# A gated mixture-of-experts layer on one core: input transposes one product earlier, the first matrix looked up early, and silu as one ScalarE function

## The chip, the cores and the metric

The kernel runs on one core of one Trainium2 chip. A core has five engines that run side by side, each with its own queue of instructions taken in order: TensorE (PE in the profile) multiplies matrices and transposes, VectorE (DVE) and ScalarE (ACT) work element by element, GpSimd (POOL) issues the gathers and scatters here, and SyncE (SP) issues the plain transfers. An engine that waits for another one's result holds up everything behind it in its own queue. The metric is the device time of one execution in microseconds (us); less is better.

## The reference, cut to what matters

```python
# x: 4 x 512 tokens of 512 values; ctx: 4 experts, each one 512 x 512 matrix
n = layernorm(x)
e = token_id // 6250, at most 3                 # each token has one of 4 experts
g = silu(n @ ctx[e].T)                          # silu(z) = z * sigmoid(z)
u = n @ ctx[e].T                                # the same matrix: u is the z of the line above
x = x + tanh(g_xattn) * ((g * u) @ ctx[e].T)    # and once more the same matrix

n = layernorm(x)
p = softmax(n @ wr.T)                           # 8 routes
gates = the two largest of p, divided by their sum
h = silu(n @ w1.T); h = silu(h @ w3.T); h = h @ w2.T
out = zeros; out[index of route k] += gate_k * h
x = x + tanh(g_ffn) * out
```

The rows of `out` are indexed by route number (0 to 7) and not by token, so the second half touches only the first eight rows of x. It still has to run over all 2048 tokens, because every token adds to those eight rows.

## The kernel before, in words

**Sorting the tokens.** The 2048 tokens are ordered by expert, so that 128 tokens (one pass) can be multiplied by one expert's matrix. A chain of small VectorE operations on `cum`, `hot`, `incl`, `size`, `cut`, `padded`, `lanes` and `what` finds each token's place in that order. Sixteen small matmuls then turn the places into `tok`, and `from_row` says which row of x each place of each pass takes. This is the position chain. There are 17 passes: 13 use one matrix each, and four, the ones numbered 13 to 16, are split into four groups of 32 rows with a matrix for each group. `matrix_table(n0, n1)` works out from `cut` which matrix each pass or group needs and puts it into `which`; the matrix of a pass can only be loaded once SyncE has read its entry of `which`.

**One pass of the expert half.** Each step below is a function of the kernel and takes the pass number:

- `gather(p)`: GpSimd collects the 128 rows of x into the tile `x` (256 KB).
- `load(p)`: SyncE reads `which` and loads the matrix `m` (1 MB), or four of them.
- `centre(p)`: VectorE takes mean and variance (`st`, `mv`) and subtracts the mean, giving `h_a`. `scale(p)` works out the inverse root `rs` by nine tiny VectorE operations. `norms(p_in, p_out)` does both for a later pass `p_in` together with the second normalization (`h_f`) of an earlier pass `p_out`.
- `turn_in(p)`: TensorE transposes `h_a` into `tp_a`, and ScalarE copies that out of PSUM as `hT`.
- `up(p)`: TensorE multiplies `hT` by the matrix into `z`; the activation is then applied and gives `g`.
- `turn_mid(p)`: TensorE transposes `g` into `tp_g`, ScalarE copies it as `gT`.
- `down(p)`: TensorE multiplies `gT` by the same matrix into `y`; VectorE adds it to `x`, and GpSimd scatters the rows back.
- `turn_out(p)`: TensorE transposes `h_f` into `tp_f`; ScalarE copies that into `hT2`, the input of the second half.

In `up`, the before kernel uses three operations, since g * u is sigmoid(z) * z * z:

```python
nc.scalar.activation(g, z, AF.Sigmoid, scale=rs)
nc.vector.scalar_tensor_tensor(g, z, rs, g, ALU.mult, ALU.mult)
nc.vector.scalar_tensor_tensor(g, z, rs, g, ALU.mult, ALU.mult)
```

**The second half.** `ffn(b)` works on a block of 512 tokens, as a generator that hands back control after each product. It makes four products `u` (by w1), the routing product `lg`, `route` (VectorE, with two small ScalarE sigmoids), four products `v` (by w3), and then `acc`, which adds up gate times h over all tokens. The last block feeds `accT` and finally `o`, the product by w2.

**Order of the work.** Nothing is scheduled automatically: the order in which the code issues is the order in each engine's queue. The main loop runs over i, the passes in the order `order`, and in each turn issues the product z of pass i, the product y of pass i - 1, the transpose of pass i - 2 for the second half, up to two pieces of `ffn` by `step()`, `turn_mid` of pass i and `turn_in` of pass i + 1. Until the first block of 512 tokens is complete (turns 2 to 5), `step()` has nothing to give.

**Buffers.** Eight matrices `m`, five tiles `x` (a tile is free again when its scatter has landed), four PSUM tiles for products, three PSUM tiles for transposes, four tiles `h` shared by `h_a` and `h_f`.

Of the kernel before, what the change touches and what calls it, by code (L numbers as in the profile page):

```python
# [8 lines left out]
F32 = mybir.dt.float32  # L9
BF16 = mybir.dt.bfloat16  # L10
F16 = mybir.dt.float16
I32 = mybir.dt.int32
AF = mybir.ActivationFunctionType
ALU = mybir.AluOpType
AX = mybir.AxisListType
# [3 lines left out]
P = 128  # L19
# [5 lines left out]
def tile_gated_moe_ffn(  # L25
# [40 lines left out]
    nc = tc.nc  # L66
    NT, D = x.shape
# [24 lines left out]
    def ct_(shape, dtype, name):  # L92
        return const.tile(list(shape), dtype, tag=name, name=name)
# [136 lines left out]
        nc.vector.tensor_reduce(padded, terms.rearrange("p h e j -> p j (h e)"), AX.X, ALU.add)  # L230
    inpass_i = ct_([P, NJ], I32, "inpass_i")
    nc.vector.tensor_single_scalar(inpass_i, padded, -P, op=ALU.bitwise_and)
    lanes = ct_([P, NJ], BF16, "lanes")
    nc.vector.tensor_sub(lanes, padded, inpass_i)
    atlane = ct_([P, 2, P, H], F16, "atlane")

    def at_lane(h):
# [44 lines left out]
                which[:, n0:n1], stepped[:, :, n0:n1].rearrange("p e n -> p n e"), AX.X, ALU.add  # L282
            )

    matrix_table(0, 2)
    from_row = ct_([P, NP], I32, "from_row")
    nc.vector.tensor_scalar(from_row, tok, -1.0, 0.0, ALU.add, ALU.max)

    first = ct_([P, NU - NF], I32, "first")
    to_row = ct_([P, NP], I32, "to_row")  # L290
# [33 lines left out]
    def moments(xt, name):  # L324
        st = small.tile([P, 6], F32, tag="st", name=f"st_{name}")
        nc.vector.bn_stats(st, xt)  # L326
        mv = small.tile([P, 2], F32, tag="mv", name=f"mv_{name}")
        nc.vector.bn_aggr(mv, st)
        return mv
# [53 lines left out]
    def centre(p):  # L383

        mvs[p] = moments(xs[p], f"a{p}")
        hs[p] = work.tile([P, D], F32, tag="h", bufs=4, name=f"h_a{p}")
        nc.vector.tensor_scalar(hs[p], xs[p], mvs[p][:, 0:1], None, ALU.subtract)  # L387
# [14 lines left out]
    def load(p):  # L402

        n0, n = (p, 1) if p < NF else (NF + (p - NF) * G, G)
        mats[p] = []
        for i in range(n0, n0 + n):
            at = nc.values_load(
                which[0:1, i : i + 1],
                engines=[SP],
                min_val=0,  # L410
                max_val=(E - 1) * D,
                skip_runtime_bounds_check_because="an expert's number, times D",
            )
            m = mp.tile([P, KC, D], F32, tag="m", name=f"m_{i}")
            nc.sync.dma_start(m, ctxT[bass.ds(at, D), :].rearrange("(k p) f -> p k f", p=P))
            mats[p].append(m)

    def expert_product(out_ps, lhs, p):

        n = P // len(mats[p])  # L420
        for k in range(KC):
            for i, m in enumerate(mats[p]):
                nc.tensor.matmul(  # L423
                    out_ps[i * n : (i + 1) * n, :],
                    lhs[:, k * P + i * n : k * P + (i + 1) * n],
                    m[:, k, :],
                    start=(k == 0),
                    stop=(k == KC - 1),
                )

    def up(p):
        z = ps_mm.tile([P, D], F32, tag="mm", name=f"z_{p}")
        expert_product(z, hTs.pop(p), p)
        g = work.tile([P, D], F32, tag="g", name=f"g_{p}")
        rs = rss.pop(p)
        nc.scalar.activation(g, z, AF.Sigmoid, scale=rs)  # L436
        nc.vector.scalar_tensor_tensor(g, z, rs, g, ALU.mult, ALU.mult)  # L437
        nc.vector.scalar_tensor_tensor(g, z, rs, g, ALU.mult, ALU.mult)  # L438
        gs[p] = g

# [21 lines left out]

    def norms(p_in, p_out):

        names, mv = [], []
        if p_out is not None:
            xt = x1s.pop(p_out)
            mv.append(moments(xt, f"f{p_out}"))
            names.append(f"f{p_out}")
        if p_in is not None:  # L470
            mv.append(moments(xs[p_in], f"a{p_in}"))
            names.append(f"a{p_in}")
        rs = inverse_roots(mv, names)
        if p_out is not None:
            h = work.tile([P, D], F32, tag="h", bufs=4, name=f"h_f{p_out}")
            nc.vector.tensor_scalar(h, xt, mv[0][:, 0:1], rs[0], ALU.subtract, ALU.mult)
            hs2[p_out] = h
        if p_in is not None:
            rss[p_in] = rs[-1]
            hs[p_in] = work.tile([P, D], F32, tag="h", bufs=4, name=f"h_a{p_in}")  # L480
            nc.vector.tensor_scalar(hs[p_in], xs[p_in], mv[-1][:, 0:1], None, ALU.subtract)

    def turn_out(p):

# [19 lines left out]
    def route(b, lg):  # L504

        def st(name, shape=(P, TT, NR)):
            return small.tile(list(shape), F32, tag=name, name=f"{name}_{b}")

        def wide(a):
            return a.unsqueeze(2).to_broadcast([P, TT, NR])

        def first_max(src, i):  # L520
            mx = st(f"mx{i}", (P, TT))
            nc.vector.tensor_reduce(mx, src, AX.X, ALU.max)
            oh = st(f"oh{i}")
            nc.vector.tensor_tensor(oh, src, wide(mx), ALU.is_equal)
            nc.vector.tensor_mul(oh, oh, rank)
            rk = st(f"rk{i}", (P, TT))
            nc.vector.tensor_reduce(rk, oh, AX.X, ALU.max)
            nc.vector.tensor_tensor(oh, oh, wide(rk), ALU.is_equal)
            return mx, oh

        lt = small.tile([P, TT, Q], F32, tag="lt", bufs=2, name=f"lt_{b}")
        nc.vector.transpose(lt.rearrange("p t q -> p (t q)"), lg)
        l1 = lt[:, :, 0:NR]
        m1, oh1 = first_max(l1, 1)
        l2 = st("l2")
        nc.vector.scalar_tensor_tensor(l2, oh1, -1e30, l1, ALU.mult, ALU.add)
        m2, oh2 = first_max(l2, 2)
        d = st("d", (P, TT))
        nc.vector.tensor_sub(d, m1, m2)
        p1 = st("p1", (P, TT))  # L540
        nc.scalar.activation(p1, d, AF.Sigmoid)
        p2 = st("p2", (P, TT))
        nc.scalar.activation(p2, d, AF.Sigmoid, scale=-1.0)
        g = small.tile([P, TT, Q], F32, tag="g", bufs=2, name=f"g_{b}")
        nc.gpsimd.memset(g, 0.0)
        nc.vector.tensor_tensor(oh1, oh1, wide(p1), ALU.mult)
        nc.vector.tensor_tensor(oh2, oh2, wide(p2), ALU.mult)
        nc.vector.tensor_add(g[:, :, 0:NR], oh1, oh2)
        return g

    def ffn(b):
# [3 lines left out]
        for m in range(KC):  # L555
            u = ps_mm.tile([P, TB], F32, tag="mm", name=f"u_{b}_{m}")
            for k in range(KC):
                nc.tensor.matmul(  # L558
                    u,
                    w1[:, k, m * P : (m + 1) * P],  # L560
                    hT[:, k, 0:TB],
                    start=(k == 0),
                    stop=(k == KC - 1),
                )
            sg = work.tile([P, TB], F32, tag="sg", name=f"sg1_{b}_{m}")
            nc.scalar.activation(sg, u, AF.Sigmoid)  # L566
            nc.vector.tensor_mul(s1[:, m, :], sg, u)  # L567
            yield
        lg = ps_tp.tile([P, P], F32, tag="tp", name=f"lg_{b}")
        for k in range(KC):  # L570
# [11 lines left out]
        def gated(t):  # L582
            v = ps_mm.tile([P, D], F32, tag="mm", name=f"v_{b}_{t}")
            for k in range(KC):
                nc.tensor.matmul(  # L585
                    v,
                    s1[:, k, t * P : (t + 1) * P],
                    w3[:, k, :],
                    start=(k == 0),
                    stop=(k == KC - 1),  # L590
                )
            s2 = work.tile([P, D], F32, tag="s2", bufs=5, name=f"s2_{b}_{t}")
            nc.scalar.activation(s2, v, AF.Sigmoid)  # L593
            nc.vector.tensor_mul(s2, s2, v)  # L594
            return s2

        def add(t, s2):
# [55 lines left out]
                step()  # L653

    load(order[0])
    load(order[1])
    for i in range(5):
        gather(order[i])
    centre(order[0])
    turn_in(order[0])  # L660
# [5 lines left out]
    wr = load_w(wrT, "wr")  # L666
    load(order[3])
    row_tables()
    centre(order[2])
    scale(order[2])  # L670
    up(order[0])
    turn_in(order[1])
    up(order[1])
    turn_mid(order[0])
    turn_in(order[2])
    down(order[0])
    turn_mid(order[1])
    norms(order[3], order[0])
# [3 lines left out]
    for i in range(2, NP + 2):  # L682
        if i < NP:
            up(order[i])
        if i + 3 < NP:
            gather(order[i + 3])
            load(order[i + 3])
        if i <= NP:
            down(order[i - 1])
        else:  # L690
            step()
        turn_out(order[i - 2])
        if i <= NP:
            norms(order[i + 2] if i + 2 < NP else None, order[i - 1])
        step()
        running += [ffn(b) for b in range(NB) if last[b] == i - 2]
        if i < NP:
            turn_mid(order[i])
        if i + 1 < NP:
            turn_in(order[i + 1])  # L700
        step()
    while running:
        step()
# [58 lines left out]
```

## Time and profile before

| | |
|---|---|
| time, median of 3 runs | 299.35 us (299.25 to 299.53) |
| span of the profiled execution | 297.4 us |
| TensorE busy | 271.3 us, 91% |
| VectorE busy | 158.4 us, 53% |
| ScalarE busy | 64.1 us, 22% |
| GpSimd busy | 38.6 us, 13% |
| granted TensorE clock | 0.993 |
| moved by DMA | 42.54 MB, mean 143 GB/s |

The span is the time from the first to the last instruction on the core; the run's time is about 2 us more. Busy shares are averages over the whole span, and this kernel has stages that differ: a start of about 20 us in which TensorE has hardly anything to do, the turns without pieces of the second half, a long middle with them, and an end that is only the second half. So the shares alone don't tell what a change is worth. The chain of waits that ended last and the idle time in front of each group are of more use.

The main groups on TensorE are z (63.6 us), y (61.8 us), u (57.0 us) and v (57.1 us), each made of 128 x 512 products. On VectorE the activation's two multiplications in `up` take 12.7 and 12.8 us, those of the second half 11.0 us each.

### The profile page before, as it was taken

What the parts mean: (1) busy time and instruction counts of PE and PEld (TensorE: products, weight loads), DVE (VectorE), ACT (ScalarE), POOL (GpSimd) and SP (SyncE); (2) the same over time, 40 slices, a digit from 0 to 9 for tenths busy, and PEclk for the clock granted to TensorE, in tenths of its full rate; (3) what the DMA queues carried; (4) which work ended last, traced back from release to release, by engine and by line L of the source; (5) the groups of instructions that cost most, each with busy time, mean ns of one, the idle gap of its engine ahead of it and who ended that gap; (6) DMA issues with size and microseconds to landing.
All of it is one profiled execution on the core that took longest, in us unless ns stands there. A gap on an engine that the chain in (4) does not pass through costs nothing.

```text
span 297.4 us, 3491 instructions
## 1 busy us (share of the span) xinstructions
PE 271.3 (91%) x1150; PEld 125.8 (42%) x1150; DVE 158.4 (53%) x610; ACT 64.1 (22%) x125; POOL 38.6 (13%) x61
## 2 busy tenths in 40 slices
PE   0148989889999999999999999999999999999994
PEld 0123444445453535443435444435443444344443
DVE  5368486877472866463755487363635543112411
ACT  1012330322121222131212221212312122111210
POOL 5420111222111111120211111010101100000000
PEclk9999999999999999999999999999999999999997
DMA  0385999994251419751429654125000000000000
GB/s 1 132 327 191 393 392 393 390 322 160 99 178 35 181 43 357 272 176 37 176 59 390 240 181 133 55 109 206 35 2 36 10 2 0 0 0 0 2 0 3
DMA packets 20722, 42.54 MB, mean 143 GB/s; under 512 B 2143, under 2 KB 2207, under 8 KB 20704
## 3 DMA queue, kind: packets, MB, share of 16 engines
q1 hardware_dynamic: 17664, 33.66, 31.6%
q0 software_dynamic: 2720, 8.65, 8.2%
q8 instruction: 9, 0.15, 0.2%
q14 instruction: 9, 0.07, 0.1%
q10 hardware_dynamic: 320, 0.01, 0.1%
HBM read 38.10 MB, written 4.47 MB: 143 GB/s over the span
## 4 chain that ended last, share of the span: by engine, by line
PE 88%; ACT 4%; issue 3%; DMA 2%; POOL 1%; DVE 1%; ACTq 0%; POOLq 0%
PE z L423 21%; PE y L423 20%; PE v L585 19%; PE u L558 19%; PE tp_f L366 3%; DMA x<-in_x_dram,from_row 2%; PE tp_a L366 2%; PE tp_g L366 2%; PE lg L573 1%; ACT hT L399 1%; PE acc L598 1%; ACT hT L490 1%; ACT gT L444 1%; POOL lane L142 1%; PE o L712 0%
## 5 line engine op out<-in xcount | busy, mean ns | idle before, releaser
L423 PE MATMUL z<-m,hT 128*32 128x512 f32 (+1 forms) x232 | 63.6, 604 | 4.4 <-ACT hT L399 4.4
L423 PE MATMUL y<-m,gT 128*32 128x512 f32 (+1 forms) x232 | 61.8, 596 | 0.4 <-ACT gT L444 0.4
L558 PE MATMUL u<-hT,w 128*128 128x512 f32 x128 | 57.0, 594 | 0.2 <-ACT hT L490 0.2
L585 PE MATMUL v<-w,s 128*128 128x512 f32 x128 | 57.1, 595 | 0.0
L423 PEld LDWEIGHTS z<-m,hT 128*32 128x32 f32 (+1 forms) x232 | 23.6, 148 | 37.5 <-issue 31.3
L423 PEld LDWEIGHTS y<-m,gT 128*32 128x32 f32 (+1 forms) x232 | 23.1, 145 | 36.7 <-issue 36.1
L558 PEld LDWEIGHTS u<-hT,w 128*128 128x128 f32 x128 | 23.4, 190 | 26.7 <-issue 26.2
L585 PEld LDWEIGHTS v<-w,s 128*128 128x128 f32 x128 | 23.4, 190 | 26.6 <-issue 24.7
L453 POOL DMA_INDIRECT out_dram<-x,to_row x17 | 16.9, 997 | 119.5 <-DVE x L452 118.9
L437 DVE SCALAR_TENSOR_TENSOR g<-z,rs_a,g 128x512 f32<-128x512 f32 x17 | 12.7, 750 | 33.0 <-ACT g L436 33.0
L594 DVE TENSOR_TENSOR s<-s,v 128x512 f32<-128x512 f32 x16 | 11.0, 686 | 30.4 <-ACT s L593 30.4
L375 POOL DMA_INDIRECT x<-in_x_dram,from_row x17 | 16.6, 977 | 74.4 <-issue 19.5
L567 DVE TENSOR_TENSOR s<-sg,u 128x512 f32<-128x512 f32 x16 | 11.0, 686 | 28.2 <-ACT sg L566 28.2
L452 DVE SCALAR_TENSOR_TENSOR x<-y,tg,x 128x512 f32<-128x512 f32 x17 | 12.8, 751 | 23.4 <-PE y L423 23.4
L436 ACT ACTIVATE g<-z,rs_a 128x512 f32<-128x512 f32 x17 | 11.7, 687 | 47.4 <-PE z L423 47.4
L566 ACT ACTIVATE sg<-u 128x512 f32<-128x512 f32 x16 | 9.6, 599 | 47.3 <-PE u L558 47.3
L366 PE MATMUL tp_a<-ident,h_a 128*128 128x128 f32 x68 | 10.7, 282 | 8.2 <-DVE h_a L387 8.2
L593 ACT ACTIVATE s<-v 128x512 f32<-128x512 f32 x16 | 9.6, 598 | 39.2 <-PE v L585 39.2
L490 ACT COPY hT<-tp_f 128x512 f32<-128x512 f32 x13 | 7.6, 586 | 43.3 <-PE tp_f L366 43.3
L326 DVE BATCH_NORM_STATS2 st_a<-x 128x6 f32<-128x512 f32 x17 | 11.3, 666 | 7.0 <-DMA x<-in_x_dram,from_row 7.0
L438 DVE SCALAR_TENSOR_TENSOR g<-z,rs_a,g 128x512 f32<-128x512 f32 x17 | 12.8, 751 | 0.6
L399 ACT COPY hT<-tp_a 128x512 f32<-128x512 f32 (+1 forms) x18 | 10.2, 573 | 13.2 <-PE tp_a L366 13.2
(132 smaller groups left out, 205.3 us busy)
## 6 DMA issues: line engine op xcount, KB each, us to landing
m<-in_ctxT_dram SPq DMA_DIRECT2D x29, 1024.0 KB
w<-in_w1T_dram SPq DMA_DIRECT2D x1, 1024.0 KB
w<-in_w3T_dram SPq DMA_DIRECT2D x1, 1024.0 KB
w<-in_w2T_dram SPq DMA_DIRECT2D x1, 1024.0 KB
x<-in_x_dram,from_row POOLq DMA_INDIRECT x17, 6.1
out_dram<-x,to_row POOLq DMA_INDIRECT x17, 5.3
wr<-in_wrT_dram SPq DMA_DIRECT2D x1, 64.0 KB
x_first<-out_dram SPq DMA_DIRECT2D x4, 4.0 KB
```

The lines of the kernel that those rows point to most:

```text
L326: nc.vector.bn_stats(st, xt)
L366: nc.tensor.transpose(tp[:, k * P : (k + 1) * P], h[:, k * P : (k + 1) * P], ident)
L375: nc.gpsimd.indirect_dma_start(out=xt, out_offset=None, in_=x, in_offset=bass.IndirectOffsetOnAxis(ap=from_row[:, p : p + 1], axis=0),)
L399: nc.scalar.copy(hT[:, i * n : (i + 1) * n], tp[:, i * n : (i + 1) * n])
L423: nc.tensor.matmul(out_ps[i * n : (i + 1) * n, :], lhs[:, k * P + i * n : k * P + (i + 1) * n], m[:, k, :], start=(k == 0), stop=(k == KC ...
L436: nc.scalar.activation(g, z, AF.Sigmoid, scale=rs)
L437: nc.vector.scalar_tensor_tensor(g, z, rs, g, ALU.mult, ALU.mult)
L438: nc.vector.scalar_tensor_tensor(g, z, rs, g, ALU.mult, ALU.mult)
L452: nc.vector.scalar_tensor_tensor(xt, y, tg[:, 0:1], xt, ALU.mult, ALU.add)
L453: nc.gpsimd.indirect_dma_start(out=out, out_offset=bass.IndirectOffsetOnAxis(ap=to_row[:, p : p + 1], axis=0), in_=xt, in_offset=None, bou ...
L558: nc.tensor.matmul(u, w1[:, k, m * P : (m + 1) * P], hT[:, k, 0:TB], start=(k == 0), stop=(k == KC - 1),)
L585: nc.tensor.matmul(v, s1[:, k, t * P : (t + 1) * P], w3[:, k, :], start=(k == 0), stop=(k == KC - 1),)
```

## The change

There are three parts.

**Transposes.** `turn_in` of the next pass moves from the end of a loop turn to directly behind `up`. For that its input must be there earlier, so the centring of a pass moves out of `norms` and forward by one place (`centre(order[i + 2])` in turn i, on VectorE between the activation of pass i and the addition of y). For the first two passes, `up` takes a function `inside` that is issued before the last quarter of the product: the second pass's `turn_in` goes inside the first z, the first pass's `turn_mid` inside the second z.

**First matrix.** The first pass's matrix number is worked out in two VectorE operations (`start`, `which0`) in the middle of the position chain. The table of the first two entries (`matrix_table(0, 2)`) moves behind `from_row`, and the second matrix is loaded after the first two gathers have been issued in program order.

**Silu.** x * sigmoid(x) becomes one ScalarE function. In `up` this takes away one of the two multiplications on VectorE, in `ffn` the only one after each u and v. The two routing sigmoids become one tanh and two small VectorE operations, since sigmoid(d) = 0.5 + 0.5 tanh(d / 2).

```diff
@@ position chain
+    start = ct_([P, 2 * E - 1], F32, "start")
+    nc.vector.scalar_tensor_tensor(start, cut[:, 1 : 2 * E], 0.0, steps, ALU.is_le, ALU.mult)
     lanes = ct_([P, NJ], BF16, "lanes")
     nc.vector.tensor_sub(lanes, padded, inpass_i)
+    which0 = ct_([P, 1], I32, "which0")
+    with nc.allow_low_precision("whole numbers below 4096"):
+        nc.vector.tensor_reduce(which0, start, AX.X, ALU.add)
...
-    matrix_table(0, 2)
     from_row = ct_([P, NP], I32, "from_row")
     nc.vector.tensor_scalar(from_row, tok, -1.0, 0.0, ALU.add, ALU.max)
+    matrix_table(0, 2)
@@ load
-                which[0:1, i : i + 1],
+                which0[0:1, :] if p == order[0] else which[0:1, i : i + 1],
@@ expert_product, up
-    def expert_product(out_ps, lhs, p):
+    def expert_product(out_ps, lhs, p, inside=None):
...
         for k in range(KC):
+            if k == KC - 1 and inside is not None:
+                inside()
...
-        nc.scalar.activation(g, z, AF.Sigmoid, scale=rs)
-        nc.vector.scalar_tensor_tensor(g, z, rs, g, ALU.mult, ALU.mult)
+        nc.scalar.activation(g, z, AF.Silu, scale=rs)
         nc.vector.scalar_tensor_tensor(g, z, rs, g, ALU.mult, ALU.mult)
@@ norms
-            mv.append(moments(xs[p_in], f"a{p_in}"))
+            mv.append(mvs.pop(p_in))
...
-            hs[p_in] = work.tile([P, D], F32, tag="h", bufs=4, name=f"h_a{p_in}")
-            nc.vector.tensor_scalar(hs[p_in], xs[p_in], mv[-1][:, 0:1], None, ALU.subtract)
@@ route
+        half = st("half", (P, TT))
+        nc.scalar.activation(half, d, AF.Tanh, scale=0.5)
         p1 = st("p1", (P, TT))
-        nc.scalar.activation(p1, d, AF.Sigmoid)
+        nc.vector.tensor_scalar(p1, half, 0.5, 0.5, ALU.mult, ALU.add)
         p2 = st("p2", (P, TT))
-        nc.scalar.activation(p2, d, AF.Sigmoid, scale=-1.0)
+        nc.vector.tensor_scalar(p2, half, -0.5, 0.5, ALU.mult, ALU.add)
@@ ffn
-            sg = work.tile([P, TB], F32, tag="sg", name=f"sg1_{b}_{m}")
-            nc.scalar.activation(sg, u, AF.Sigmoid)
-            nc.vector.tensor_mul(s1[:, m, :], sg, u)
+            nc.scalar.activation(s1[:, m, :], u, AF.Silu)
...
-            nc.scalar.activation(s2, v, AF.Sigmoid)
-            nc.vector.tensor_mul(s2, s2, v)
+            nc.scalar.activation(s2, v, AF.Silu)
@@ start of the work
     load(order[0])
+    for i in range(2):
+        gather(order[i])
     load(order[1])
-    for i in range(5):
+    for i in range(2, 5):
         gather(order[i])
...
+    up(order[0], inside=lambda: turn_in(order[1]))
     centre(order[2])
     scale(order[2])
-    up(order[0])
-    turn_in(order[1])
-    up(order[1])
-    turn_mid(order[0])
+    up(order[1], inside=lambda: turn_mid(order[0]))
     turn_in(order[2])
+    centre(order[3])
     down(order[0])
@@ main loop
         if i < NP:
             up(order[i])
+        if i + 1 < NP:
+            turn_in(order[i + 1])
+        if i + 2 < NP:
+            centre(order[i + 2])
...
             turn_mid(order[i])
-        if i + 1 < NP:
-            turn_in(order[i + 1])
         step()
```

## The prediction

> **What bounds the kernel now.** I read the page's slices first, then who waited for whom, then the chain that ended last, then single engines in order of time.
>
> ```profile
> PE   0148989889999999999999999999999999999994
> DMA  0385999994251419751429654125000000000000
> ```
>
> Each digit is a slice of 7.4 us. TensorE is full from about 75 us to the end. It has holes in slices 1 to 10 only: nothing a faster VectorE or ScalarE does in the middle can count. DMA is full around 35 to 67 us.
>
> ```profile
> PE tp_a L366 <- DVE h_a L387: 8.2, 1, 8.2
> PE z L423 <- ACT hT L399: 4.4, 6, 0.8
> PE acc L598 <- DVE s L594: 0.4, 1, 0.4
> PE y L423 <- ACT gT L444: 0.4, 1, 0.4
> ```
>
> TensorE's own waits (total, times, longest): one long one at the start, six of up to 0.8 us in which z waits for the copy of its transposed input, and two of 0.4 us. Apart from the start, TensorE waits little over 5 us in 297.
>
> ```profile
> 10.57 6.12 DMA x<-in_x_dram,from_row
> ...
> 19.83 5.44 PE z L423 x8
> 25.27 0.02 issue
> 25.30 0.46 ACT g L436
> 25.75 0.13 issue
> 25.88 0.59 ACT hT L399
> 26.47 0.04 issue
> 26.51 3.71 PE z L423 x8
> ...
> 43.91 0.60 ACT hT L399
> 44.52 0.04 issue
> 44.56 3.70 PE z L423 x8
> ...
> 257.19 0.61 ACT s L593
> 257.82 0.70 DVE s L594
> ```
>
> This is the chain that ended last (start, length). The start hangs on the first gather, 6.12 us. From 71 to 212 us the chain is TensorE alone. A product after a wait takes 3.70 us, one without 3.43: 0.27 us is lost to refilling besides the wait. The first z takes 5.44.
>
> ```profile
> 12.00:13.00 1.00, 0.00 (x0) 0.00 (x0) 0.00 (x0) 0.00 (x0) 0.95 (x1) 1.00 0.65 186
> 13.00:14.00 1.00, 0.00 (x0) 0.00 (x0) 0.00 (x0) 0.00 (x0) 0.74 (x1) 1.00 1.04 397
> 15.00:16.00 1.00, 0.00 (x0) 0.00 (x0) 0.00 (x0) 0.00 (x0) 0.69 (x2) 1.00 0.99 361
> ```
>
> The last two columns of the stretches by engine are DMA share and GB/s. From 11 to 16.7 us about 1.65 MB moved (61, 186, 397, 399, 361 and two thirds of 371 KB), though the gathered tile is 0.26 MB: it came in behind the first matrix, 1.05 MB. A gather issued at 90.1 us, with no matrix moving, landed in 3.4 us.
>
> **The Trainium skill.** "ScalarE: Activation LUTs", on what happens when an ACTIVATE runs, has one element per cycle and lane whatever the function, so Silu should cost what Sigmoid does. The trace shows Sigmoid at 599 ns for 512 elements, 687 ns with the scale from a tile; Silu isn't in it. The same page ("What ACT_TABLE_LOAD costs") gives 1283 ns for a load; the trace has two, of 1283 ns each. The changed order has two as well: tanh and Silu share the second, so no switching arises. "DMA: Bandwidth & Descriptors", in "Issuing engines are not separate DMA queues", says transfers from all issuers run on the same 16 engines and interleave; that agrees with the 6.12 against 3.4 us above. "TensorE: Matmul & The Clock Gate", in "What's actually happening", puts an idle array at half clock until about 3.4 us of activity in a free-running window; the first z's weight loads indeed come 0.85 us apart until about 23.3 us and 0.43 after.
>
> **The change part by part.**
>
> *First matrix.* `which` now ends at 9.85 us and the matrix is issued at 10.55, 0.7 later. `which0` would end near 7.2 us, so the issue goes to about 7.9, and at the same delays its megabyte is in by about 12.8. The two added operations (0.17 us each, like their neighbours on `lanes`) stand partly in gaps between dependent neighbours: 0 to 0.2 us on the path, I take 0.1. Moving `matrix_table(0, 2)` behind `from_row` saves nothing, since it ran while `from_row` waited 0.25 us for `tok`. It delays the second matrix to about 11.6 us, which helps: the first gather, issued at 10.65, finds the engines nearly free. Bounds: 3.4 us as at 90.1, landing at 14.05; or mixed with the second matrix, up to 15.2. I take 14.2 against 16.69: gain 2.5 us. The first z follows 3.15 us after landing, as now (16.69 to 19.83), at 17.35. Its matrix is there.
>
> *Second z.* Now 25.27 to 26.51 is 1.24 us, of which the transposes are 0.44. With the transpose inside the first z, ScalarE copies during the last quarter (0.86 us; copy 0.58 plus 0.04). Gain 1.24 - 0.44 + 0.27 = 1.1 us. The second input must be centred by 21.7 us; it should land near 16.
>
> *First y.* Now 30.23 to 31.46, 1.23 us, less two transposes 0.88, plus 0.27: 0.6 us. A new wait eats part: the table load (1.28 us) now stands on ScalarE behind the copy of the second `hT`, so silu of the first pass starts 1 us after its product, and multiplication (0.75) and `tp_g` follow. With the transposes done at 22.05 us: copy to 22.7, load to 23.95, silu to 24.7, multiplication to 25.45, transposes at 25.6, against 25.5 when TensorE gets there. Behind it on VectorE the centring of the third pass (1.42 us) ends near 26.9, when TensorE wants it. So about 0.3 us is lost; gain 0.3 (0 to 0.6).
>
> *Turns 3 to 5.* z waits at 44.56, 53.79 and 63.01, each with 0.78 us idle plus 0.27. Now z, `tp_a` of the next pass, y, `tp_f` and `tp_g` follow without a gap, since `hT` is copied during y: 3.43 + 0.44 + 3.43 + 0.44 + 0.44 = 8.18 us a turn against 9.23. Gain 3 x 1.04 = 3.1 us.
>
> *The last split pass.* z at 215.23 us waits 0.73 because its input's copy queues behind four copies to `hT2`. It will have been copied a turn before. Gain 0.8 with the refill. The 0.24 us wait of u at 223.61 stays: `hT2` is copied in the same place.
>
> *Silu.* 17 multiplications of 0.75 and 32 of 0.69 us leave VectorE, 34.8 us, beside TensorE's work nearly everywhere. On the path are two: before `acc` at 258.56, where u follows 0.7 us sooner; and before the last `accT`, where 0.7 us falls away but `accT` now queues behind the transposes of `a`, which end near 290.75, so it starts there and not at 291.07: 0.3 us. Routing gets two operations of about 0.15 us in place of a ScalarE one; `acc` needs its result over 6 us later.
>
> Sum: 2.5 + 1.1 + 0.3 + 3.1 + 0.8 + 0.7 + 0.3 = 8.8 us, 299.35 - 8.8 = 290.5 us.
>
> **A new wait.** `centre` of pass i + 2 now waits on VectorE for its gather in turn i, ahead of the addition of y. A gather waits for a scatter to free its tile, so the loop is: y added, scatter (6.2 to 6.9 us while DMA is full), gather (6.1 to 6.9), centring. From y added at 31.8 us I get the sixth x at about 45.2, where VectorE would take it at 44.5; the seventh at 53.2 against 52.6. Behind the wait stands the addition of y, whose product ends at 46.8 and 55.0, and the centring takes 1.42. So 0.5 to 0.7 us of waiting fits in, with about a microsecond to spare; from turn 6 a turn takes 15 us and it vanishes.
>
> **The rivals.**
>
> A: the first gather lands no earlier, because the second matrix or the other four gathers take the engines. For it: 6.1 to 6.7 us for all five gathers now. Against it: the bytes that moved before it landed are those of the first matrix. Only the waits go: 299.35 - 6.3 = 293.0.
>
> B: the gather loop becomes the bound in turns 3 to 5, with VectorE late by more than the spare time. For it: DMA full in these slices. Against: the sums above. Losing two thirds of the turns' gain, 2.1 us: 292.6.
>
> C: `tp_a` directly behind z makes TensorE wait in the long middle, where it has no wait now. With 1 us in each of the 11 turns from the seventh on: 290.5 + 11 = 301.5, slower. Against: the centring it needs is a turn old, some 15 us, and VectorE has lost a fifth of its work.
>
> **How the numbers follow.** The forecast 72%, A 12%, B 11%, C 5%. The forecast itself may move by the clock ramp: the first z comes 2.5 us earlier against a free-running window, and could run longer or shorter at half clock, -0.6 to +1.2 us; the gather adds -0.2 to +1.0, the table load 0.3 either way. So 288.7 to 293.3: the forecast's spread with A and B, leaving out C and little of the rest. Faster 0.95 (forecast, A, B), slower 0.04 and the same 0.01, both from C.
>
> **What would show it.** Right: the first gather in under 4.2 us; first z near 17.4 us; no wait of z for `hT` from turn 3 on, products of 3.43 us in the chain; the stretch from the first z to the first u about 47 us in place of 51.5; Silu at 599 and 687 ns. Wrong: a gather still near 6 us (A); VectorE waiting over 1.5 us for x in turns 3 to 5, with y's addition late (B); TensorE waiting for `h_a` after 75 us (C); a third table load.

## The result and the profile after

The changed kernel takes 291.42 us (median of four runs, 291.08 to 293.33) against 299.40 us for the kernel before on the same chip: a ratio of 0.975 [0.971, 0.979]. The profiled span went from 297.4 to 289.6 us, 7.80 us less.

TensorE's row of the page's slices, of the kernel after (a slice is 7.2 us):

```profile
PE   0159999999999999999999999999999999999994
```

The 8s that stood among the first 9s before are gone: TensorE is at 9 from the fourth slice to the last but one. VectorE's busy time fell from 158.4 to 128.8 us.

TensorE's waits after (who waited for whom: total us, times, longest):

```profile
PE tp_a L372 <- DVE h_a L393: 7.0, 1, 7.0
...
PE u L565 <- ACT hT L495: 0.5, 2, 0.2
PE z L431 <- ACT hT L405: 0.5, 1, 0.5
```

Six waits of z for its transposed input (4.4 us) have become one, the first z's. The waits of `acc` and of y are gone. The wait at the start fell only from 8.2 to 7.0. And u now waits twice where it waited once: that one is new.

The chain that ended last, after (start and length in us; x6 is the first six of the eight passes that make a 128 x 512 product; where transposes now stand inside a product they divide it, so the 3.52 us from 23.47 on are the last two passes of the first z and the first six of the second):

```profile
10.75 4.78 DMA x<-in_x_dram,from_row
...
16.50 0.64 DVE h_a L393
...
18.83 4.20 PE z L431 x6
23.04 0.44 PE tp_a L372 x4
23.47 3.52 PE z L431 x8
26.99 0.60 PE tp_g L372 x4
27.60 0.86 PE z L431 x2
28.46 0.54 PE tp_a L372 x4
...
32.87 3.44 PE z L431 x8
...
41.05 3.44 PE z L431 x8
...
57.41 3.44 PE z L431 x8
...
64.72 0.45 PE tp_f L372 x4
65.20 0.59 ACT hT L495
65.83 3.70 PE u L565 x8
69.54 3.43 PE z L431 x8
```

Two readings carry the rest. The four z from 32.87 us on stand 8.18 us apart, products of 3.44 us with one y and nothing else but transposes of 0.44 between them. And the first u at 65.83 is a product of 3.70 us, the mark of one that had to wait: the chain passes through ScalarE's copy `hT` at L495 (the tile that the text calls `hT2`).

Where the 7.80 us of span came from, by the positions of the same instruction in both chains (the difference of one row less that of the row above):

| up to | before | after | gained in this part |
|---|---|---|---|
| first z | 19.83 | 18.83 | 1.00 |
| third z | 35.60 | 32.87 | 1.73 |
| the z behind the first u | 74.96 | 69.54 | 2.69 |
| last split z | 215.23 | 208.95 | 0.86 |
| u behind the third block's `acc` | 259.61 | 252.54 | 0.79 |
| last result, `ob` | 293.89 | 286.09 | 0.73 |

### The profile page after: what moved, and what is told of

Its sections match the earlier page's. It is cut to its first block, busy times and chain, and to the rows that moved or that the text cites. A ratio compares the mean times of both kernels' runs of the same rounds, so it can differ in the third digit from the quotient of the medians.

```text
span 289.6 us, 3462 instructions
## 1 busy us (share of the span) xinstructions
PE 269.1 (93%) x1150; PEld 124.8 (43%) x1150; DVE 128.8 (44%) x571; ACT 63.7 (22%) x121; POOL 38.6 (13%) x61
## 2 busy tenths in 40 slices
DMA packets 20722, 42.54 MB, mean 147 GB/s; under 512 B 2143, under 2 KB 2207, under 8 KB 20704
## 4 chain that ended last, share of the span: by engine, by line
PE 93%; DMA 3%; DVE 2%; ACT 1%; issue 0%; DVEq 0%
PE z L431 21%; PE y L431 20%; PE u L565 19%; PE v L590 19%; PE tp_a L372 3%; PE tp_f L372 3%; PE tp_g L372 2%; DMA x<-in_x_dram,from_row 2%; PE acc L602 2%; PE lg L578 1%; DMA idt<-in_ids_dram 1%; PE accT L612 1%; PE tok L264 0%; ACT hT L495 0%; PE o L719 0%
## 5 line engine op out<-in xcount | busy, mean ns | idle before, releaser
L445 DVE SCALAR_TENSOR_TENSOR g<-z,rs_a,g 128x512 f32<-128x512 f32 x17 | 12.8, 750 | 63.7 <-ACT g L444 63.7
L431 PEld LDWEIGHTS y<-m,gT 128*32 128x32 f32 (+1 forms) x232 | 22.5, 146 | 27.9 <-issue 27.9
L460 POOL DMA_INDIRECT out_dram<-x,to_row x17 | 16.9, 996 | 116.7 <-DVE x L459 116.1
L572 ACT ACTIVATE s<-u 128x512 f32<-128x512 f32 x16 | 9.6, 597 | 47.2 <-PE u L565 47.2
L537 DVE STREAM_TRANSPOSE lt<-lg 128x128 f32<-128x128 f32 x4 | 1.3, 316 | 37.2 <-PE lg L578 37.2
L495 ACT COPY hT<-tp_f 128x512 f32<-128x512 f32 x13 | 7.6, 586 | 42.7 <-PE tp_f L372 42.7
L372 PEld LDWEIGHTS tp_a<-ident,h_a 128*128 128x128 f32 x68 | 8.4, 145 | 16.7 <-issue 14.9
L372 PEld LDWEIGHTS tp_f<-ident,h_f 128*128 128x128 f32 x68 | 8.2, 141 | 10.2 <-issue 10.2
```

The source lines that it names most:

```text
L372: nc.tensor.transpose(tp[:, k * P : (k + 1) * P], h[:, k * P : (k + 1) * P], ident)
L431: nc.tensor.matmul(out_ps[i * n : (i + 1) * n, :], lhs[:, k * P + i * n : k * P + (i + 1) * n], m[:, k, :], start=(k == 0), stop=(k == KC ...
L460: nc.gpsimd.indirect_dma_start(out=out, out_offset=bass.IndirectOffsetOnAxis(ap=to_row[:, p : p + 1], axis=0), in_=xt, in_offset=None, bou ...
L572: nc.scalar.activation(s1[:, m, :], u, AF.Silu)
```

## Experiments

Each changes the kernel after, unless said otherwise. "Trace" is that of one profiled execution; times are medians of four to six runs, and the kernel before took 299.5 to 299.6 us on the same chips.

### 1. The kernel after once more

> The changed kernel itself, unaltered, for its spread. Its four runs gave 291.08, 291.33, 291.51 and 293.33 us. If the 293.33 was one disturbed run, these stay within 291.0 to 291.8. If the kernel itself has two ways to start (the first gather mixing with the second matrix in another order), more runs near 293 turn up.

Measured: 291.58 us (291.29, 291.29, 291.88, 292.71), ratio 0.973 [0.972, 0.975]. The profiled execution was the one of 292.71. From its chain:

```profile
10.76 5.17 DMA x<-in_x_dram,from_row
...
19.08 5.33 PE z L431 x6
```

The same six passes took 5.33 us here and 4.20 above, and 1.13 us is most of the distance to the other runs (the gather took another 0.39). In the trace the weight loads of the first z stand 0.85 us apart until about 24 us here, until about 21.6 in the other execution, and 0.43 apart afterwards. The Trainium skill, "TensorE: Matmul & The Clock Gate", section "What's actually happening", describes this: an array that was idle is at half clock until a free-running window of about 3.4 us has seen it busy. The spacing of the loads agrees; the profile's column of the granted clock doesn't show it, it reads 1.00 there in both executions. So two executions of one kernel differ by a microsecond, and differences below that need the trace's positions besides the medians. (The 293.33 us of the first four runs has no trace, so its cause isn't shown.)

### 2. First matrix looked up where it was before

```diff
-    start = ct_(...)
-    nc.vector.scalar_tensor_tensor(start, cut[:, 1 : 2 * E], 0.0, steps, ...)
...
-    which0 = ct_([P, 1], I32, "which0")
-        nc.vector.tensor_reduce(which0, start, AX.X, ALU.add)
...
+    matrix_table(0, 2)
     nc.vector.tensor_scalar(from_row, tok, -1.0, 0.0, ALU.add, ALU.max)
-    matrix_table(0, 2)
...
     load(order[0])
-    for i in range(2):
-        gather(order[i])
     load(order[1])
-    for i in range(2, 5):
+    for i in range(5):
         gather(order[i])
```

> The changed kernel with the first matrix looked up as before: no start and which0, the two-entry table ahead of from_row, all five gathers after the second load. Theory: the gather waits behind the first matrix, so x lands near 16.9 us in place of 15.54 and everything after moves by that: about 1.1 to 1.3 us slower than the changed kernel, 292.5. Rival: the landing is set by the five gathers among themselves and the early lookup brought nothing: no change, 291.4.

With the lookup, the second matrix's load goes back ahead of the gathers in the program. Measured: 293.23 us (292.52 to 293.51), 0.979 [0.978, 0.981]. Its chain:

```profile
10.76 6.16 DMA x<-in_x_dram,from_row
...
20.07 4.15 PE z L426 x6
```

The gather takes 6.16 us again, as before the change (6.12). The first z starts 1.24 us after that of the kernel after and runs equally long; the medians are 1.65 apart. So the early lookup is worth between 1.2 and 1.7 us, and not the 2.5 forecast.

### 3. The second matrix later

Its table entry is worked out behind the first centring, and it is loaded after all five gathers.

```diff
     nc.vector.tensor_scalar(from_row, tok, -1.0, 0.0, ALU.add, ALU.max)
-    matrix_table(0, 2)
...
     load(order[0])
-    for i in range(2):
-        gather(order[i])
-    load(order[1])
-    for i in range(2, 5):
+    for i in range(5):
         gather(order[i])
     centre(order[0])
+    matrix_table(0, 2)
+    load(order[1])
     turn_in(order[0])
```

> The changed kernel with the table of the first two entries, and so the second matrix's load, moved behind the centring of the first pass; the early first matrix stays. Theory 1 (the second matrix's packets mix with the gather's): x lands 0.5 to 0.9 us sooner, 14.6 to 15.0, 290.8. Theory 2 (as forecast, a gather with the engines to itself takes 3.4 us): x lands at 14.15, 1.4 us sooner, 290.0. Rival (the tail of the first matrix alone holds the gather): x lands at 15.4 or later, 291.4. The second matrix would then arrive near 20 us, before the second z at 24.3.

Measured: 291.47 us (291.37 to 291.66), 0.973 [0.972, 0.975]: no faster than the kernel after. From its chain, and from its list of waits:

```profile
10.79 3.46 DMA x<-in_x_dram,from_row
...
16.92 7.43 DMA m<-in_ctxT_dram
...
24.49 2.81 PE z L430 x6
```

```profile
PE z L430 <- DMA m<-in_ctxT_dram: 1.2, 1, 1.2
```

The gather takes 3.46 us and lands at 14.25, where the forecast had put it for the kernel after. The first z starts at 17.62 us. But the second matrix, issued at 16.92 behind four more gathers, lands at 24.35, where about 20 had been expected, and the second z waits for it. What the gather gains is lost one product later. It settles two things: the lookup did free the first gather from the first matrix, and what still delayed it in the kernel after is the second one.

### 4. The second matrix behind the second gather

The number of the second matrix is copied by GpSimd, whose queue reaches the copy only after it has issued two gathers; the load on SyncE waits for the copy.

```diff
                 which0[0:1, :] if p == order[0] else
+                which1[0:1, :] if p == order[1] else
                 which[0:1, i : i + 1],
...
     for i in range(2):
         gather(order[i])
+    which1 = ct_([P, 1], I32, "which1")
+    nc.gpsimd.tensor_copy(which1, which[:, 1:2])
     load(order[1])
```

> The changed kernel with the second matrix's number handed to SyncE by a small GpSimd copy behind the second gather, so that its load is issued near 14 us, between the 11.6 of the changed kernel and the 17 of the run with the load behind the centring. Theory (the load, once queued, costs the first gather 1.3 us; issued behind it, it costs nothing and still arrives before the second z): x lands at 14.3, first z starts near 17.6, no wait for a matrix, 1.3 us faster, 290.1. Rival (the bytes come to the same total, so the second z waits for the matrix by what the first gained): 291.4.

Measured: 290.62 us (289.78 to 290.68), 0.970 [0.968, 0.972]. Its chain:

```profile
10.74 3.68 DMA x<-in_x_dram,from_row
...
17.65 4.61 PE z L431 x6
```

The gather takes 3.68 us, and no product waits for a matrix. The first z starts 1.18 us sooner than after, of which the clock took 0.41 back (4.61 against 4.20); the median is 0.8 to 1.0 below the two of the kernel after. Together with the run above this shows the *order* of matrix and gather in time to be what counts: that matrix was issued at about 11.5 us in the kernel after, 13.8 here and 16.9 in experiment 3. Two microseconds later is enough to free the gather, five are too late for the second product.

### 5. Sigmoid and multiplication again, transposes as changed

```diff
-        nc.scalar.activation(g, z, AF.Silu, scale=rs)
+        nc.scalar.activation(g, z, AF.Sigmoid, scale=rs)
+        nc.vector.scalar_tensor_tensor(g, z, rs, g, ALU.mult, ALU.mult)
...
-            nc.scalar.activation(s1[:, m, :], u, AF.Silu)
+            sg = work.tile([P, TB], F32, tag="sg", name=f"sg1_{b}_{m}")
+            nc.scalar.activation(sg, u, AF.Sigmoid)
+            nc.vector.tensor_mul(s1[:, m, :], sg, u)
...
-            nc.scalar.activation(s2, v, AF.Silu)
+            nc.scalar.activation(s2, v, AF.Sigmoid)
+            nc.vector.tensor_mul(s2, s2, v)
```

> The changed kernel with sigmoid and the VectorE multiplications back in all three places; routing stays with tanh. Theory: only what stands on the path counts: 0.70 us before the last product of acc, 0.3 at the end, 0.78 in the second z, whose transposes of g wait for one multiplication more: 1.8 us slower, 293.2. Rival (VectorE would be the bound in turns 3 to 5, where it also waits for the gathers): over 3 us slower, with y added late and z or tp_a waiting.

Measured: 294.14 us (293.95 to 294.31), 0.982 [0.981, 0.984], 2.6 us slower than the run of the kernel after beside it. The waits that came back:

```profile
PE tp_g L372 <- DVE g L446: 0.7, 1, 0.7
...
PE acc L606 <- DVE s L602: 0.4, 1, 0.4
```

The turns stay at 8.18 us (z at 34.36, 42.54, 50.72, 58.90): nearly all of the 49 multiplications that VectorE got back cost nothing, and the turns' gain isn't Silu's. By positions in the chain, against the kernel after: 0.71 us at the first z (the gather and the clock), 0.78 by the third z (`tp_g` waits), 0.72 at `acc`, 0.40 at the last result. The middle two and the last, 1.9 us, are what Silu is worth; 1.8 had been expected. The product `o` took 1.12 us here too.

### 6. Transposes back in their old places, Silu and first matrix as changed

```diff
-    up(order[0], inside=lambda: turn_in(order[1]))
...
-    up(order[1], inside=lambda: turn_mid(order[0]))
+    up(order[0])
+    turn_in(order[1])
+    up(order[1])
+    turn_mid(order[0])
...
             up(order[i])
-        if i + 1 < NP:
-            turn_in(order[i + 1])
-        if i + 2 < NP:
-            centre(order[i + 2])
...
             turn_mid(order[i])
+        if i + 1 < NP:
+            turn_in(order[i + 1])
```

The centring goes back into `norms` as well.

> The changed kernel with the transposes and the centring where they were before (norms as before, nothing inside a product, turn_in at the end of a turn); early first matrix and silu stay. Theory: the six waits of z come back, 0.8 to 0.9 idle and 0.27 of refill each, and with them the waits of the second z and first y, while the new wait of the first u (0.4) goes: 1.7 + 2.7 + 0.8 = about 5.0 us slower, 296.4. Rival: silu alone shortened the ScalarE and VectorE chain, so the waits come back smaller: 3 us slower or less.

Measured: 297.02 us (296.39 to 297.76), 0.992 [0.989, 0.995], 5.4 us slower than the kernel after. Its waits at z, y and u are those of before:

```profile
PE z L431 <- ACT hT L405: 4.3, 6, 0.8
...
PE y L431 <- ACT gT L451: 0.4, 1, 0.4
...
PE u L567 <- ACT hT L497: 0.2, 1, 0.2
```

So the moved transposes, with the centring that goes with them, are the largest part of the change, about two thirds of it, and u's second wait comes with them: here there is one wait of 0.2 us, after the change two.

### 7. One table load instead of two

A Silu of two elements stands ahead of the tanh at the start, so that Silu's set is loaded there, and tanh uses it.

```diff
     tg = ct_([P, 2], F32, "tg")
+    early = ct_([P, 2], F32, "early")
+    nc.scalar.activation(early, gates, AF.Silu)
     nc.scalar.activation(tg, gates, AF.Tanh)
```

> The changed kernel with a silu of the two gate values ahead of the first tanh, so that the one table that holds both is loaded at the start and the load in front of the first pass's silu falls away. Theory: that load (1.28 us on ScalarE, from 24.11) makes the transposes of g inside the second z 0.16 us late, with 0.1 for the next transposes: 0.2 to 0.3 us faster, 291.1. Rival (tp_g then waits for VectorE, which ends its tables at 24.93): no gain, 291.4.

Measured: 291.72 us (291.37 to 291.87), 0.974 [0.972, 0.975], no gain in the median. In the trace one table load is left, at the start, and the transposes after it run without a wait:

```profile
18.93 4.89 PE z L433 x6
...
24.26 3.52 PE z L433 x8
27.78 0.44 PE tp_g L374 x4
28.22 0.86 PE z L433 x2
29.08 0.44 PE tp_a L374 x4
```

`tp_g` took 0.60 and `tp_a` 0.54 in the kernel after, 0.44 each here. From the end of the transposes inside the first z to the start of the third z it is 9.13 us (24.26 to 33.39) against 9.40 (23.47 to 32.87). So 0.27 us is there in the trace, and the first z at its slower clock (4.89 against 4.20) covers it.

### 8. The second half's transpose ahead of y in every turn

Meant against the new wait of u: with the products of y behind it, `tp_f` is copied in time.

```diff
             load(order[i + 3])
+        turn_out(order[i - 2])
         if i <= NP:
...
             step()
-        turn_out(order[i - 2])
```

> The changed kernel with turn_out ahead of down in every turn, so that y stands between the transposes of h_f and the u that needs their copy. Theory: both waits of u for that copy (0.24 us at 65.6 and at 217, each with 0.27 of refill) go: 0.8 to 1.0 us faster, 290.5. Rival (h_f isn't ready so early; in turn 3 it ends at 44.41 us and TensorE comes at 44.92): new waits of tp_f for h_f in turns 2 to 5 eat the gain: 291.4 or slower.

Measured: 293.17 us (292.23 to 293.47), 0.979 [0.977, 0.981]: slower than the kernel after. The chain shows a turn:

```profile
41.36 3.44 PE z L431 x8
44.80 0.44 PE tp_a L372 x4
45.30 0.63 PE tp_f L372 x4
45.92 3.44 PE y L431 x8
...
49.80 3.44 PE z L431 x8
```

u doesn't wait any more, but `tp_f` starts 0.06 us late and takes 0.63 us in place of 0.44, since its input `h_f` comes out of VectorE only then: 8.44 us a turn in place of 8.18, in four turns. Near the end one `tp_f` waits a whole 0.5 us for `h_f`. The rival's reason holds: the transpose stood late because its input is late.

### 9. The same, only where u follows

```diff
+        begins = i - 2 in (last[0], last[2])
+        if begins:
+            turn_out(order[i - 2])
         if i <= NP:
...
-        turn_out(order[i - 2])
+        if not begins:
+            turn_out(order[i - 2])
```

> The changed kernel with turn_out ahead of down in turns 5 and 16 only, the two whose u waits for the copy of h_f's transposes. Theory: in the other turns the forward place made those transposes wait for h_f; in these two h_f is ready, both waits of 0.24 us and their refills go: 0.8 to 0.9 us faster, 290.6. Rival (tp_f waits for h_f here too): 291.4.

Measured: 290.95 us over six runs (290.32 to 292.78), 0.973 [0.971, 0.976]. No wait of u is left in the list of waits and none of `tp_f` comes in. From its chain:

```profile
33.22 3.44 PE z L431 x8
...
65.95 3.44 PE u L565 x8
```

The first u starts 32.73 us after the third z (33.22 to 65.95) against 32.96 after (32.87 to 65.83), and is 0.26 us shorter (3.44), 0.5 us in all. With the second u, from the third z to the y behind it, it is 187.05 us against 188.10: 1.05 us, what had been expected for both and a little more. The median is only 0.5 below, with a first z of 4.50 us against 4.20, and the interval is too wide to show it: this one stands on the trace.

### 10. Three parts together: second matrix by SyncE late, one table, transpose first

The edits of experiments 3, 7 and 8.

> The changed kernel with one table load, turn_out ahead of down and the second matrix behind the first pass's centring, all three. If their gains add: 0.6 + 0.3 + 0.9 = 1.8 us faster, 289.6, below both kernels. If one of them takes over another's wait: between 290 and 291.

Measured: 292.51 us (291.91 to 292.81), 0.976 [0.974, 0.978], 2.9 us above what had been expected. Each part brought its own cost along: the turns 8.44 us long, a wait of 0.8 us ahead of the second z, and the first z at half clock for longer (six passes 5.19 us).

### 11. The better three: second matrix by GpSimd, one table, transpose first where u follows

The edits of experiments 4, 7 and 9.

> The changed kernel with the second matrix by the GpSimd copy, one table load, and turn_out ahead of down in turns 5 and 16. If the three gains add, 1.3 + 0.3 + 0.9 = 2.5 us faster: 288.9. If the start's gains fall into TensorE's half-clock ramp, whose end doesn't move with the first z: 289.5 to 290.5.

Measured: 289.13 us (288.89 to 290.05), 0.966 [0.964, 0.968], as expected within 0.3. The gains read from the traces of experiments 4, 7 and 9, 1.18 + 0.27 + 1.05 = 2.5 us, add up to the 2.3 to 2.5 measured, once none of them takes its cost along. Two of the five runs, 289.84 and 290.05, lie where the other expectation had them; in the trace, that of the 290.05, the first six passes took 5.21 us.

### 12. And the clock warmed up

Experiment 11 with 13 products of 128 x 512 in bf16 behind the position chain's matmuls, whose result nobody reads.

```diff
+    warm = ps_mm.tile([P, TB], F32, tag="mm", name="warm")
+    for i in range(13):
+        nc.tensor.matmul(warm, ones, lane[:, 0:64, :]..., start=True, stop=True)
     which = ct_([P, NU], I32, "which")
```

> The run before it, with 13 products of 128 x 512 bf16 added on TensorE between tok and the first transposes, whose result nobody reads. Theory (the spread between runs of one kernel, and 1.6 to 2.7 us of the first z, are TensorE at half clock until some microseconds of work): the first three quarters of the first z take 2.6 us in place of 4.2 to 5.3, its transposes 0.5 in place of 1.1; 2.3 to 3.3 us faster than the run before it, 286 to 286.6, and the runs agree within 0.4 us. Rival (the first z is slow for another reason, such as its matrix still arriving): no gain.

Measured: 288.12 us (287.93 to 288.43), 0.963 [0.961, 0.964], the best of all, and its runs agree within 0.5 us. From the stretch of TensorE's timeline (start, length; in brackets the idle time before and what ended it):

```profile
10.10 4.39 PE L272 MATMUL warm<-lane,ones 128*128 128x512 bf16 x13
16.12 0.63 PE L379 MATMUL tp_a<-ident,h_a 128*128 128x128 f32 x4 [1.63 <-DVE h_a L400]
17.21 2.84 PE L438 MATMUL z<-m,hT 128*128 128x512 f32 x6 [0.46 <-ACT hT L412]
...
22.23 2.81 PE L438 MATMUL z<-m,hT 128*128 128x512 f32 x6 [0.88 <-DMA m<-in_ctxT_dram]
```

The first six passes take 2.84 us, the first transpose 0.63 where it was 1.10. So what the other runs took beyond that, 4.15 to 5.33 us, was the half clock and not a matrix that was still arriving. Only 1.0 of the expected 2.3 us or more showed in the time: the first z now ends before the second matrix is in, and the second z waits 0.88 us for it. That the clock makes the spread between runs as well isn't shown by the 0.5 us: such a wait would even out differences in the first z, and experiment 3, with a wait of 1.2 us at the same place and no warm-up, has runs within 0.3 us.

## Why the prediction was right, and where it wasn't

*What bounds the kernel.* Right. TensorE's few waits at the start and in the turns carried nearly all that was gained; experiment 6 gives 5.4 us back with the transposes alone, experiment 5 1.9 us with Silu, experiment 2 1.2 to 1.7 with the lookup. They add up to 8.5 to 9.0, against 8.0 measured. The first six passes differ by up to 1.2 us between these traces (4.15 to 5.33), enough to account for the rest, but that isn't separated here.

*First matrix*, 2.5 forecast, 1.00 measured: the term that was mis-sized. The two added operations cost nothing on the path (from the start of `inpass_i` to that of `atlane` 0.50 us before, 0.49 after), and the first matrix was early, as said. But the forecast took 14.2 us for the gather's landing, between bounds of 14.05 and 15.2, on the reading that the second matrix comes later, at 11.6 us, and that this "helps". It was issued at 11.46 us, and before at 11.47: nothing was delayed. The gather landed at 15.53, outside even the upper bound, after 4.78 us instead of the 3.55 forecast. Experiments 3 and 4 show the cause: with the second matrix issued later, the gather took 3.46 and 3.68 us. The queues show how (q1 carries the matrices, q0 the gathers; packets, MB, share of the 16 engines' time). From 12.5 to 13.5 us, first in the kernel after, then in experiment 4:

```profile
q1 hardware_dynamic: 57, 0.11, 64.0%
```

```profile
q0 software_dynamic: 54, 0.22, 86.2%
q1 hardware_dynamic: 8, 0.01, 3.7%
```

By 12.5 us the first matrix was in (1.04 MB moved). In the microsecond that followed, the kernel after moved 0.11 MB of the second matrix and nothing of the gather, although the gather had been issued 0.7 us ahead of it; in experiment 4 the gathers had this time to themselves. It is the same in every trace with the early lookup: none of the gather in this microsecond in the seven runs with the second matrix at 11.5 us, 0.20 to 0.22 MB in the five with it at 13.8 or later. From 14 to 15 us, in the kernel after, the two shared the engines evenly:

```profile
q1 hardware_dynamic: 88, 0.18, 47.6%
q0 software_dynamic: 54, 0.18, 44.1%
```

The Trainium skill, "DMA: Bandwidth & Descriptors", section "Queues, rings and completion order", says that an engine alternates between its queues packet by packet; this agrees with the even shares from 14 us on, not with the microsecond ahead of it. Few bytes moved then, 0.11 MB where it had been 0.40 from 11 to 12 us, and yet the second matrix's packets took 64% of the engines' time for them (40 to 106% in the other six runs). Why they take so long, and why the gather's packets don't start meanwhile, stays open. The trace of before had a hint of all this: of the 1.65 MB that the forecast counted ahead of the gather's landing, the first matrix and the gathered tile are only 1.31, and the rest was in the main the second matrix (q1 moved 1.37 MB in that stretch). The remainder of the miss is 0.14 us of `h_a`, 0.64 us against 0.50 before, and 0.10 of a later issue: in this trace, and in every one of the changed kernels, the first transfer, of the token numbers, lands 0.18 us later than in the one of before, for a reason that isn't known.

*Second z* and *First y*, 1.1 + 0.3 forecast, 1.73 measured. The table load did cost its 0.3 (`tp_g` 0.16 and `tp_a` 0.10 longer, shown by experiment 7). The other 0.3 is the clock, by what the first z took: in before's trace the first z's eight passes took 5.44 us, two of them at 0.43, so six took 4.58, against 4.20 after.

*Turns 3 to 5*, 3.1 forecast, 2.69 measured. The turn is 8.18 us, to the hundredth. The turns give 3.14; 0.45 of it went at the end of the last turn, which the forecast overlooked, and 2.69 are left. There `tp_a` no longer stands between `tp_f` and the first u, so u waits 0.24 us for the copy of `tp_f`, and the product takes 3.70 us where it took 3.50 before. The forecast named the wait of u at 223.61 us, which stayed, and not this one, its like. Experiment 9 takes both away, and the trace gets half a microsecond back at each.

*The new wait* of VectorE for the gathers came in two turns and was harmless, as forecast (0.5 to 0.7 us each). From VectorE's timeline of the kernel after:

```profile
46.69 0.69 DVE L332 BATCH_NORM_STATS2 st_a<-x 128x6 f32<-128x512 f32 x1 [0.69 <-DMA x<-in_x_dram,from_row]
```

It was 0.69 us here and 0.26 a turn later; the additions of y behind them still waited 0.28 and 0.71 us for their products, so nothing was late.

*The last split pass*, 0.8 forecast, 0.86 measured. *Silu* at `acc`, 0.7 forecast, 0.79 measured. Its prices are Sigmoid's, 687 and 597 ns, as forecast, and the trace has two table loads again. From the page's groups of the kernel after (busy us, mean ns of one, idle time before):

```profile
L444 ACT ACTIVATE g<-z,rs_a 128x512 f32<-128x512 f32 x17 | 11.7, 687 | 38.3 <-PE z L431 38.0
L572 ACT ACTIVATE s<-u 128x512 f32<-128x512 f32 x16 | 9.6, 597 | 47.2 <-PE u L565 47.2
```

*The tail*, 0.3 forecast, 0.73 measured. The last `accT` starts behind the transposes `tp_sum`, as forecast: from the u of the table to the start of `o` it is 32.40 us against 32.80. The remaining 0.3 is `o`, 1.12 us against 1.46. In before's windows the granted clock (the column ahead of DMA share and GB/s) was

```profile
293.00:294.00 1.00, 0.84 (x20) 0.39 (x8) 0.11 (x1) 0.00 (x0) 0.00 (x0) 0.50 0.00 0
```

and in the kernel after

```profile
285.00:286.00 1.00, 1.00 (x32) 0.75 (x32) 0.00 (x0) 0.00 (x0) 0.00 (x0) 1.00 0.00 0
```

This is no merit of Silu: experiment 5, with the multiplications back, had `o` at 1.12 us too. Nor is it shown to be one of the change at all: before has only this one trace, and every run of the changed kernels has its `o` at 1.12 or 1.13.

*The rivals.* A (the gather no earlier): the gather landed 1.16 us sooner in place of 2.5, so A is half true, and by its own reason, the second matrix. B (the gather loop bounds the turns) and C (`tp_a` waits in the middle) are refuted: turns of 8.18 us, with Silu and, in experiment 5, without; no wait of `tp_a` in the list but the first.

Of the signs named ahead, two failed, both of the first matrix: a gather under 4.2 us (4.78) and a first z near 17.4 (18.83). The others came: no wait of z for `hT` from turn 3 on, products of 3.44 us, 47.0 us from the first z to the first u, and Silu's prices.

The sum came out 0.9 us low because one term was 1.5 too large and one loss of 0.45 was overlooked, while the clock gave some 0.7 back, at both ends of the kernel. That the measured time lies well inside the range is in part luck: the gather landed 1.3 us late, more than the 1.0 that the range allowed for it, and the 0.7 from the clock was no merit of the working.

## What to carry to other kernels

Work moved one product earlier was worth here the wait it removed, plus the 0.27 us of refilling behind it, where its input was already there; where the input is made just in time, as `h_f` in experiment 8, the same move makes a new wait. Look at what stood between a transpose and its reader before anything is moved away from there. And when a load is brought forward, ask what moves up behind it: the second matrix was issued at the same time as before, but with the first one out of the way its bytes came next, ahead of the gather that starts everything. The queues of the profile before show such a candidate, if the bytes are counted by queue.

## What the runs showed of the hardware that was not expected

- A gather of 262 KB took 6.1 to 6.2 us behind a matrix of 1.05 MB, 4.8 to 5.2 with another matrix issued 0.7 us after it, and 3.5 to 3.9 when that matrix was issued three microseconds or more after it. In the second case the bytes of the later matrix went first, from 12.5 to 13.5 us, though the DMA engines moved only 0.10 to 0.14 MB in that microsecond.
- The first six passes of the first product took 4.15 to 5.33 us, differently from run to run, against 2.84 after 4.4 us of products that nobody reads, which ended 1.6 us before the first transposes. The granted clock of the profile reads 1.00 in the slow stretch too.
- The granted clock fell to half during the last product, `o`, in the one trace of before (1.46 us against 1.12). Of the other traces, those that show a fall at the end show it after `o`.
